# Attention's rounds: parts turned ahead of the projection, their copies ahead of the exponentials, small copies dealt to other engines

## The chip, the core and the metric

The kernel runs on one core of a Trainium2 chip. The metric is the device time in microseconds (us), the median of several runs; before the change it is 1904.55 us (three runs, 1902.47 to 1905.32). The engines are named as the profile names them: PE is the matrix engine, PEld its loading of weights, DVE the vector engine, ACT the scalar engine, POOL GpSimd, SP the queue that issues the transfers.

## What is computed

A hybrid block of transformer parts, all in float32, on x of 4 x 256 tokens with 512 features:

```python
x = x + attention(layernorm(x))   # 32 heads of 16, rotary, causal, plus 10 adapter keys and values
x = x + ffn(layernorm(x))         # x @ weight.T + bias, kept only where clusters are hit
x = x + ssd_mixer(layernorm(x))   # in_proj, conv of 4 taps, state-space mixer of 128 heads, gate, norm, out_proj
x = x + ffn(layernorm(x))         # the same weights again
return x
```

In attention, queries and keys are projected and rotated, `scores = q k / 4` are masked causally, a softmax follows, and its weights meet the values. The adapter's keys and values, projected with the same weights from 10 rows, add a second, separate softmax times a gate. The sum goes through `w_proj`. The change lies in attention and in the first feed-forward, which is woven into attention's last rounds. The mixer, which takes most of the time, is not edited.

## The kernel before, in words

**Precision.** A product in float32 is made of three matmuls [...]: each operand is split into a high half (a rounded copy) and a low half (the rest). `split` (L102) makes the two, the high one on ACT (L104), the low one on DVE or POOL (L105). `mm3` (L107) issues the three matmuls for each of 4 blocks of 128 features (L112 to L114), so a projection of one tile of 128 tokens is 12 matmuls. 16 numbers of a head are stacked as high and low halves to a depth of 64, so that scores come from single matmuls on "parts".

**Attention's rounds.** The loop of L658 has 32 rounds, i = 0 to 31. Each is four heads (u = i mod 8) of one batch (b = i div 8), and queries and keys of 256 tokens. Work of several ages meets in a round, in this order of TensorE:

1. `scores(b, u)` (L429): 8 matmuls of parts into four PSUM tiles `sc` (L443), then 4 matmuls that add the mask (L450). DVE takes the negative maxima `nmx` (L455), ACT the exponentials with their sums into `e` (L458), eight instructions.
2. In even rounds but the first the first half of `adapter_scores` (L401): 4 matmuls into `pa`; ACT copies it to `sa` (L409).
3. `step("long", i)`: projections that are due. `prepared` (L360) lists those of the next batch: two query and two key projections and two of values for its two tiles of tokens; each q or k is then rotated by DVE (L281 to L285) and summed to `r` on POOL (L287); values are copied by ACT (L385). The number `r` in `prepared` (L363) is the round at which the first of them is due, and each takes the next round. For the first batch it is negative, and what falls below zero is done ahead of the loop. Projections of attention's output (`closed`, L546) and of the feed-forward (`fed`, L583) are due in the same way.
4. Parts (second half of `pieces`, L387): 8 transposes `trp` (L395), then two copies to `pc` (L397), on DVE for queries (f = 0) and on ACT for keys (f = 1).
5. `step("values", i)`, for some rounds the adapter's values `pya` (L540).
6. `weigh` of round i-2 (L477): exponentials that were turned before, times values, to `py`; ACT copies `py` to `ys` (L494).
7. `turn` of round i-1 (L464): 12 transposes of `e` into three tiles `ptr` (L473); they are copied to `eT` (L474), the first two on DVE and the third on ACT.
8. `gathered` of round i-3 (L497): two transposes `try` (L500), then the division by the sums on DVE; then the second half of the adapter's scores, `tra` (L413).
9. `step("turn", i)`: transposes that are due: normalised tiles (`tr`, L163, whose halves are `axs`), output rows (`try`, L557), the adapter's weights (`pt`, L531), at the start the adapter's keys (`tra`, L336).
10. First half of `pieces` for a later round: `stacked` (L301) writes the high halves into a stack `st` with a copy that is repeated twice, on ACT (L305), and the low halves with a subtraction on POOL (L306). There are two stacks for queries and two for keys, and a part uses both of its kind; rounds alternate between queries and keys.

**PSUM.** Projections, `trp`, `pa`, `ptr`, `try`, `tra`, `tr` and the like share three buffers of tag "m". Scores have four of their own, `py` one.

**What sets the order.** On TensorE the loop's order is as written (`manual_schedule`, L657). The instructions of other engines are put in order by the framework's planner when the program is built: each has a priority from its place in the program, and among those that its own model of time has ready the earliest goes first. [...] `tc.high_priority(offset=60)` moves what is written in its block ahead in priority by 60 places.

**The stage's end.** After the loop the last rounds are finished by hand (L713 to L747): the last output projections, and the feed-forward for the tiles of tokens 3 to 7. Tiles 6 and 7 are normalised, both turned (L744), then both fed (L747).

## Time and profile before

| What | us |
|---|---|
| median of 3 runs | 1904.55 |
| the profiled execution | 1905.57 |
| its span, first to last instruction | 1903.8 |
| ahead of attention's rounds | 0 to 33 |
| rounds 0 to 31 of attention, and what follows round 31 at once | 33 to 350 |
| the rest of attention and of the first feed-forward | 350 to 385 |
| mixer and second feed-forward | 385 to 1904 |

A line of the groups view gives line, engine, operation and tiles, then busy time, the mean of one in ns, and the idle time ahead of it with what ended it. The groups that matter between 40 and 345 us, by that view:

| Group | count | mean ns |
|---|---|---|
| L458 ACT exponential, 128x256 and 128x128 | 248 | 430 |
| L458 ACT reading of the sum after each | 248 | 217 |
| L455 DVE maximum | 124 | 546 |
| L473 PE transposes of exponentials | 384 | 285 |
| L474 copies to eT: DVE, ACT | 64, 32 | 684, 597 |
| L397 copies to pc: DVE, ACT | 30, 30 | 678, 627 |
| L305 ACT copies to st | 56 | 447 |
| L306 POOL subtractions to st | 56 | 458 |
| L494 ACT copies to ys | 31 | 404 |

Matmuls overlap in the array, so the duration of one (0.39 us for 512 columns) is longer than the distance to the next (0.235 us). The distance is what counts for the sum.

### The profile page before, as it was taken

Reading aid. Unit: us, or ns where it says so; the run is one execution under the profiler, and the core shown is the slowest. Engines: PE = TensorE matmul, PEld = TensorE weight load, DVE = VectorE, ACT = ScalarE, POOL = GpSimd, SP = SyncE. Lnnn points to the kernel's source line nnn. Section 1 sums busy time; section 2 is a strip of 40 time slices with the busy share of each in tenths; the row PEclk is TensorE's granted clock in tenths of the full one; section 3 lists DMA queues with packets and bytes.
Section 4 is the critical chain, followed back from the end, with each engine's and each line's share of the span. In section 5 each row is a group of like instructions: output and inputs, shape, how many; then the busy total and the mean of one; then the engine's idle time right before and its main releaser. Section 6 shows DMA issues by size and latency. Waiting matters only on the chain.

```text
span 1903.8 us, 29900 instructions
## 1 busy us (share of the span) xinstructions
PE 1815.8 (95%) x10690; PEld 1453.8 (76%) x10690; DVE 1473.3 (77%) x2319; ACT 1379.9 (72%) x2874; POOL 346.9 (18%) x312
## 2 busy tenths in 40 slices
PE   7989888889999999999999999999999999999997
PEld 5767666767777887878788788777787888787786
DVE  5466667588998778777877797778778877877777
ACT  4676687368898767867877787678777776786753
POOL 4221120011321211121112121210221121111100
PEclk8999999999999999999999999999999999999999
DMA  3000000025555454554445454545554444455341
GB/s 132 11 1 1 22 14 1 22 66 173 171 186 180 155 166 144 162 165 150 157 159 161 144 188 137 177 144 168 150 167 142 158 155 161 147 159 170 112 124 49
DMA packets 151909, 240.35 MB, mean 126 GB/s; under 512 B 12368, under 2 KB 77520, under 8 KB 151760
## 3 DMA queue, kind: packets, MB, share of 16 engines
q1 hardware_dynamic: 151760, 238.44, 39.3%
q8 instruction: 84, 1.38, 0.3%
q14 instruction: 65, 0.53, 0.1%
HBM read 202.75 MB, written 35.65 MB: 125 GB/s over the span
## 4 chain that ended last, share of the span: by engine, by line
PE 73%; ACT 12%; DVE 8%; DMA 3%; issue 3%; POOL 1%; SPq 0%; ACTq 0%; DVEq 0%; POOLq 0%
PE pp L112 12%; PE pp L113 11%; PE pp L114 11%; PE pyy L1016 8%; PE pog L112 6%; PE pog L114 6%; PE pog L113 6%; ACT e L458 4%; PE trx L1001 3%; DMA wor<-in_wout_dram 1%; PE ptr L473 1%; DVE acc L942 1%; ACT L946 1%; PE pg L956 1%; ACT acc L946 1%
## 5 line engine op out<-in xcount | busy, mean ns | idle before, releaser
L112 PE MATMUL pp<-mx,w 128*128 128x512 f32 (+1 forms) x1160 | 465.1, 401 | 9.1 <-DVE acc L942 8.6
L114 PE MATMUL pp<-mx,w 128*128 128x512 f32 (+1 forms) x1160 | 454.1, 391 | 0.0
L113 PE MATMUL pp<-mx,w 128*128 128x512 f32 (+1 forms) x1160 | 453.9, 391 | 0.0
L942 DVE SCALAR_TENSOR_TENSOR acc<-pp,cw_s,acc 128x1012 f32<-128x1012 f32 (+2 forms) x240 | 304.9, 1270 | 22.9 <-ACT acc L935 22.3
L990 DVE TENSOR_TENSOR em<-em,gm 128x1536 f32<-128x1536 f32 x128 | 229.7, 1795 | 94.3 <-ACT em L984 86.0
L112 PEld LDWEIGHTS pp<-mx,w 128*128 128x128 f32 x1160 | 218.2, 188 | 66.9 <-issue 11.0
L114 PEld LDWEIGHTS pp<-mx,w 128*128 128x128 f32 x1160 | 218.4, 188 | 45.5 <-issue 0.4
L113 PEld LDWEIGHTS pp<-mx,w 128*128 128x128 f32 x1160 | 218.6, 188 | 40.8 <-issue 0.7
L1039 POOL TENSOR_TENSOR sq<-sq,acc 128x1024 f32<-128x1024 f32 x55 | 132.5, 2409 | 583.1 <-ACT acc L1038 583.1
L104 ACT CAST w<-wr 128x512 fp32r<-128x512 f32 x144 | 88.5, 615 | 189.0 <-PE pp L113 154.2
L978 POOL TENSOR_SCALAR_AFFINE_SELECT r<-r 128x512 f32<-128x512 f32 x128 | 125.1, 977 | 548.9 <-DMA r<-cumd 484.6
L112 PE MATMUL pog<-wo,gh 128*128 128x512 f32 x512 | 204.4, 399 | 0.0
L983 ACT ACTIVATE em<-r,col_t 128x128 f32<-128x128 f32 x512 | 164.9, 391 | 48.7 <-PE pyy L1016 48.4
L114 PE MATMUL pog<-wo,gh 128*128 128x512 f32 x512 | 200.2, 391 | 0.0
L113 PE MATMUL pog<-wo,gh 128*128 128x512 f32 x512 | 199.9, 390 | 0.0
L1016 PE MATMUL pyy<-em,xd 128*64 128x256 f32 (+1 forms) x2048 | 189.1, 329 | 2.9 <-DVE em L990 2.9
L1016 PEld LDWEIGHTS pyy<-em,xd 128*64 128x64 f32 x2048 | 134.0, 137 | 64.4 <-issue 20.4
L986 ACT ACTIVATE em<-r,col_t 128x128 f32<-128x128 f32 x512 | 166.5, 388 | 0.0
L974 DVE TENSOR_SCALAR em<-r,col_t 128x128 f32<-128x128 f32 x512 | 137.7, 328 | 12.6 <-PE pyy L1016 10.1
L1002 DVE TENSOR_TENSOR xd<-trx,dt_t 128x512 f32<-128x512 f32 x128 | 86.1, 682 | 53.7 <-PE trx L1001 53.6
L458 ACT ACTIVATE e<-sc,nmx 128x256 f32<-128x256 f32 (+1 forms) x256 | 103.5, 430 | 31.3 <-DVE nmx L455 31.3
L105 DVE TENSOR_TENSOR w<-wr,w 128x512 fp32r<-128x512 f32 x139 | 98.2, 708 | 34.5 <-ACT w L104 34.4
(287 smaller groups left out, 3187.9 us busy)
## 6 DMA issues: line engine op xcount, KB each, us to landing
wr<-in_win_dram SPq DMA_DIRECT2D x287, 256.0 KB, 2.8
r<-cumd SPq DMA_DIRECT2D x128, 512.0 KB, 4.2
spill<-gb SPq DMA_DIRECT2D x63, 512.0 KB, 2.8
gr<-spill SPq DMA_DIRECT2D x120, 256.0 KB, 3.3
wor<-in_wout_dram SPq DMA_DIRECT2D x64, 256.0 KB, 3.2
out_dram<-x SPq DMA_DIRECT2D x8, 256.0 KB, 2.3
x<-in_x_dram SPq DMA_DIRECT2D x1, 1536.0 KB, 9.5
gr<-spill SPq DMA_DIRECT2D x8, 192.0 KB, 2.6
```

What stands on the lines that cost most here:

```text
L112: nc.tensor.matmul(o, lh, rh, start=(first and k == 0), stop=False)
L113: nc.tensor.matmul(o, lh, rl, start=False, stop=False)
L114: nc.tensor.matmul(o, ll, rh, start=False, stop=(last and k == n - 1))
L458: nc.scalar.activation(es_[c][:, 2 * j + pr, :], sc[:, j, :], AF.Exp, bias=nm[:, j : j + 1], accum_out=rs[:, c, h : h + 1],)
L942: nc.vector.scalar_tensor_tensor(av[:, :, d:], pv[:, :, : L - d], cw_s[:, ch, tap : tap + 1], av[:, :, d:], ALU.mult, ALU.add,)
L974: nc.vector.tensor_scalar(e[:, b, 2, :], rv[:, b, 1, :], col_t[:, h, b, 1:2], 0.0, ALU.subtract, ALU.min,)
L978: nc.gpsimd.affine_select(rv[:, :, 0, :], rv[:, :, 0, :], pattern=[[0, B], [1, P]], compare_op=ALU.is_ge, fill=-1e30, base=0, channel_mult ...
L983: nc.scalar.activation(e[:, b, 1, :], rv[:, b, 1, :], AF.Exp, bias=col_t[:, h, b, 2:3])
L986: nc.scalar.activation(e[:, b, 0, :], rv[:, b, 0, :], AF.Exp, bias=col_t[:, h, b, 0:1])
L990: nc.vector.tensor_tensor(e, e, gm, ALU.mult)
L1016: nc.tensor.matmul(py[d, b, k * P :], xd[:, 2 * b + k, d], es2[hh][:, b, 2 * k : 2 if k == 0 else 3, :].rearrange("p s i -> p (s i)"), sta ...
L1039: (nc.gpsimd if n < NB - 1 else nc.vector).tensor_tensor(sq, sq, x2, ALU.add)
```

## The change

It has these parts, all but the last two in the rounds:

- `scores` becomes a generator: its first half ends after the maxima, its second half has the exponentials.
- In a round, the parts are turned (point 4 above) after point 2 and ahead of the exponentials and of `step("long", i)`. So the order is scores, adapter, parts, exponentials, projections, values and so on.
- Both kinds of parts are copied to `pc` by ACT.
- Of the turned exponentials, the one of the first 128 queries (first in order) is copied by ACT, the two others by DVE.
- `ys` is copied by DVE in place of ACT.
- The high halves in `stacked` are copied by POOL in place of ACT.
- The first batch's list starts at -6 in place of -5, the second's at 1 in place of 0: one value projection more is done ahead of the loop, and those of the second batch come one round later.
- In `fed`, a tile's normalising and turning get a priority that is 60 places ahead.
- At the stage's end tile 6 is turned and fed, then tile 7.

```diff
@@ stacked
-                nc.scalar.copy(st[:n, :, HI[f], :], v.to_broadcast([n, 8, 2, HD]))
+                nc.gpsimd.tensor_copy(st[:n, :, HI[f], :], v.to_broadcast([n, 8, 2, HD]))
@@ prepared
-                r = 8 * (b - 1) if b else -5
+                r = {0: -6, 1: 1}.get(b, 8 * (b - 1))
@@ pieces
-                    nc.scalar.copy(o[:, :, cs], tr) if f else nc.vector.tensor_copy(o[:, :, cs], tr)
+                    nc.scalar.copy(o[:, :, cs], tr)
@@ scores
-                made = []
+                made, tops = [], []
...
                     nc.vector.tensor_reduce(nm, sc, AX.X, ALU.max, negate=True)
+                    tops.append(nm)
+                yield
+                for (c, pr, sc), nm in zip(made, tops):
                     for j in range(2):
                         h = 4 * u + 2 * j + pr
                         nc.scalar.activation(
...
-                return es_
+                all_es[8 * b + u] = es_
+                yield
@@ turn
-                    nc.scalar.copy(dst, pt) if k else nc.vector.tensor_copy(dst, pt)
+                    nc.scalar.copy(dst, pt) if src is es_[0] else nc.vector.tensor_copy(dst, pt)
@@ weigh
-                nc.scalar.copy(ys, py)
+                nc.vector.tensor_copy(ys, py)
@@ fed
-                xs = normed(f.norm, t)
+                with tc.high_priority(offset=60):
+                    xs = normed(f.norm, t)
@@ the loop
-                    es_[i] = scores(b, u)
+                    scoring = scores(b, u)
+                    next(scoring)
...
-                    step("long", i)
                     if part:
                         next(part)
                     part = None
+                    next(scoring)
+                    step("long", i)
                     step("values", i)
...
-                        eTs[i - 1] = turn(es_.pop(i - 1))
+                        eTs[i - 1] = turn(all_es.pop(i - 1))
@@ the end
                     feed.norm.turn(xn, tr, xs)
-                    late[t] = xs
-                for t, xs in late.items():
                     feed.tile(t, xs, [ps_s.tile([P, FH], F32, name="pd", tag="sc") for _ in range(2)])
```

More of the change, by code (lines that the diff above doesn't have):

```diff
@@ L624, in attention @@
             n = B * 8
-            es_, eTs, yss = {}, {}, {}
+            all_es, eTs, yss = {}, {}, {}
             feed = None
@@ L715, in attention @@
                 yss[n - 2] = weigh(b, 6, eTs.pop(n - 2))
-                eTs[n - 1] = turn(es_.pop(n - 1))
+                eTs[n - 1] = turn(all_es.pop(n - 1))
                 gathered(b, 5, yss.pop(n - 3))
```

## The prediction

> **What bounds the kernel now.** I read the page first, its busy shares, slices and chain:

> ```profile
> PE 1815.8 (95%) x10690; PEld 1453.8 (76%) x10690; DVE 1473.3 (77%) x2319; ACT 1379.9 (72%) x2874; POOL 346.9 (18%) x312
> PE   7989888889999999999999999999999999999997
> PEclk8999999999999999999999999999999999999999
> PE 73%; ACT 12%; DVE 8%; DMA 3%; issue 3%; POOL 1%; SPq 0%; ACTq 0%; DVEq 0%; POOLq 0%
> ```

> TensorE sets the time. The slices below 9 are the first nine, and those are attention. The table by stage (us, then busy time of PE, PEld, DVE, ACT, POOL, then the clock) says how much can be won:

> ```profile
> 33.00:130.00 97.00, 86.10 (x630) 67.50 (x631) 53.73 (x110) 65.45 (x242) 24.99 (x36) 0.92 0.04 12
> 130.00:262.00 132.00, 120.69 (x1003) 94.18 (x1002) 86.73 (x187) 89.47 (x331) 28.52 (x41) 1.00 0.05 13
> 262.00:350.00 88.00, 74.50 (x659) 60.27 (x658) 60.49 (x147) 59.77 (x207) 9.88 (x16) 0.96 0.04 13
> 385.00:1904.00 1519.00, 1486.64 (x8161) 1192.40 (x8159) 1228.99 (x1762) 1137.50 (x2043) 264.10 (x191) 0.99 0.48 151
> ```

> From 33 to 350 us PE idles 35.7 of 317 us (10.9+11.3+13.5), and no other engine is full: ACT 68%, DVE 63%, POOL 20%. The mixer after 385 isn't touched. Then the waits of PE alone in 33 to 350 (total us, times, longest):

> ```profile
> PE ptr L473 <- ACT pc L397: 5.6, 5, 1.6
> PE trp L395 <- ACT sa L409: 4.5, 6, 1.0
> PE ptr L473 <- DVE pc L397: 3.6, 3, 2.0
> PE pd L112 <- ACT axs L104: 3.6, 2, 2.8
> PE tra L413 <- ACT eT L474: 3.3, 9, 0.5
> PE pya L540 <- ACT pc L397: 2.4, 2, 1.2
> ```

> Most are waits for a PSUM buffer of tag "m" (three of them) that a copy has not yet emptied, and the copy stands behind the exponentials on ACT. The timeline shows it, in round 4 (80 to 89 us) and in round 7:

> ```profile
> 84.88 0.38 ACT L409 COPY sa<-pa 80x256 f32<-80x256 f32 x1
> ...
> 85.41 0.51 PE L395 MATMUL trp<-con,st 128*128 128x128 f32 x4 [0.64 <-ACT sa L409]
> ...
> 88.90 0.36 PE L413 MATMUL tra<-con,sa 80*128 80x80 f32 x2 [0.39 <-ACT eT L474]
> ...
> 112.03 1.11 ACT L397 CAST pc<-trp 128x512 fp32r<-128x512 f32 x2
> 112.70 0.66 PE L473 MATMUL ptr<-con,e 128*128 128x128 f32 x4 [1.58 <-ACT pc L397]
> ```

> pa was complete at 81.5, but its copy came at 84.9, after eight exponentials (81.7 to 84.9), and PE lost 0.8 us. In round 7, which has no projection as cover, PE lost 1.8 us twice.

> [...] after the waits before 33 us a projection's matmuls start 0.43 us apart until 38.9, then 0.235; the same at 58 to 62 and 114 to 118 us. So a long wait costs some 2 us more afterwards. [...] L306 on POOL takes 449 to 467 ns in all 64 full-size cases[...]. [...] 128x512 from PSUM takes 681 ns on DVE (L474) and 586 on ACT.

> **The change, part by part.** A projection occupies PE for 2.8 us (81.52 to 84.32), scores and masks 1.0, a part's turning 0.75, values 0.8, the three turns of exponentials 1.45, the way back 0.35; pa and tra of even rounds 0.55 and 0.3. So a round with a projection holds 7.1 us (odd) or 8.0 us (even) of PE work. The starts of scores in the timeline (72.60, 79.98, 89.19, 96.58, 105.56, 113.51 for rounds 3 to 8) give 7.4 for odd and 9.2 and 9.0 for even rounds: the even ones have 1.0 to 1.2 us to give.

> *Order.* Turning a part right after the scores, its two copies (0.63 each on ACT) ahead of the exponentials. ACT runs sa 0.38, pc 1.25, exponentials 3.35: they end some 6.1 us (odd) or 6.5 (even) after the round's start, 1.2 to 1.5 later than now. The projection (1.75 to 4.6 us of the round) covers that. sa is empty about when the second turning ends, so the buffer for the projection is ready. Worked round by round against the starts in the timeline:
> - Even rounds with a projection: 4, 10, 12, 18, 20, 28 give 0.95 to 1.2 each (6.65), 6, 14, 22 and 30 0.15 to 0.5 (1.3): **-8.0**.
> - Rounds in which values or turns wait for pc: 9 and 17 give 1.5 each, 15 and 23 0.7, 25 0.6, 29 0.9: **-5.9**.
> - Odd rounds 3, 5, 11, 19: already near full, 0.2 to 0.35 each: -1.15. Rounds 13 and 21 project values, whose copy (0.62, ACT) comes behind the later exponentials: +0.3 each. Sum **-0.6**.
> - Rounds without a projection (8, 16, 24, 26, 27) have no cover. The late exponentials and the turn's first copy behind them (end near 7.1) hold the next buffer, unless that is taken from a DVE copy. Round 27 takes 6.25 now, 26 takes 7.8, 16 takes 8.3. I take +0.7, +0.2, +0.5, and -0.5 and -0.9 for 8 and 24, which now also pay for a cold clock or for copies ahead of their exponentials: **0**.
> - Round 2's cold clock (2 us now) halved: **-1.0**. Round 31 waits 2.8 for axs behind late exponentials; the feed's higher priority can take axs ahead: -2.5 to 0, I take **-1.0**.

> *The shifted projections* (first index -6 and 1). One value projection (2.8) goes ahead of the rounds, where PE waits 5.5 us for parts (trp on POOL's st, two waits). It hides there, but turnings then come later and the stacks (two for each of q and k) pass that on through POOL: rounds start 1.5 later. Round 0 keeps two projections, less cold: -1.0. Round 1 loses both, 5.6 of PE work, and becomes bound by ACT and the adapter's keys: -5.6+1.5. Round 7 gains one, whose 2.8 fill its 3.4 of waits: 8.4 instead of 7.95, +0.45. Sum **-3.2**.

> *Copies dealt anew*, over 32 rounds: st (64 and 4 copies) leaves ACT for POOL, -29.3 on ACT (64 x 0.433 + 4 x 0.398); the parts of q (32) go from DVE to ACT, +20.1 on ACT (x 0.628), -21.7 on DVE (x 0.678); ys (32) from ACT to DVE, -12.7 on ACT (x 0.396), about +13.1 on DVE by the 128x256 row at 0.41 (L284). ACT -21.9, DVE -8.6: off the path by themselves, their effect is in the rounds above. The turn's copies stay two DVE, one ACT, but ACT has the first. The POOL copy of 128x256 isn't in the trace: a cast of half that width took 0.29 (L610) and once 0.787 (L611), a memset of 8 columns 0.104. Taking 0.1 fixed and 0.19 for 128 columns: 0.48. [...] Ends: 0.31 (memset's rate) and 1.57 (twice 0.787). Two copies and two subtractions are 1.9 us, on an engine that now waits for ACT's st (117 us of waits). They hide, if POOL runs them in the round before: it can, since ACT now issues st as soon as the stack is free (85.14 in round 4, for a part turned two rounds later). No SP or DMA queue is moved past.

> *End of the stage.* Turn and feed of tile 6 now come ahead of tile 7's turn. PE waits 3.1 there (tr on axn), but tile 6's low half comes on DVE only at 369.97, after that axn; and tile 7's split is then no longer hidden (1.3). **0**, between -2 and +2.

> Sum -8.0-5.9-0.6-1.0-1.0-3.2 = -19.7. Copies put in places where a slot or a queue is a little late give some back; for that I take 1.7, about what PE waits now in the smaller lines of its list: **-18.0**. The profiled execution took 1905.57 (span 1903.8 and 1.8 around it): 1887.6. It lies 1.0 above the median of 1904.55, so I forecast **1887**.

> **The rivals.** *A, as worked out*: 1887, by itself 1875 to 1896; 0.62. *B, the wait is exchanged*: exponentials end 1.2 to 1.5 us later and the turn's first copy stands behind them, so the some 20 rounds with projections lose 0.6 each by a wait of try or tra for eT: -18+12, **1899**. For it: PE waits for eT already (3.3 us). Against: DVE's copies give earlier buffers. 0.20. *C, slower*: the parts are turned 2.8 us earlier in the round than now, so st must be ready 1.0 us after its start. If POOL runs the four st instructions only where they are written, at the end of the round, each of 29 rounds waits 1.9-1.0, with PE uncovered: +26-18 = +8, **1913**. It decides from 18/29 = 0.62 us a round. For it: [...] the sum r (1.28) can stand ahead. Against: the early issue above. 0.12. *D, the order of ACT stays*: only PE's order is fixed by hand; if the planner still puts exponentials first, the buffers stay late, and the shifted projections alone give 3: **1902**; 0.06.

> **How the numbers follow.** A fills 1875 to 1896; the low end 1873 adds the bounds of round 31 and the stage's end. B takes the range up to 1903, leaving out C and a little of each: about 2 in 10. A measurement can tell about 0.2% (3.8 us) from no change. Faster by more: A and most of B, 0.78. Within: rest of B and D, 0.10. Slower: C, 0.12.

> **What would show it.** Right: sa and pc stand before or among the first exponentials; PE no longer waits for sa (4.5) or pc (11.6 in three lines); even rounds take 8.0 to 8.3; L305 shows POOL at about 0.48; PE idle in the stage falls from 36 to some 20 us. B: a long line of try or tra for ACT eT. C: trp for POOL st grows past 10 us. Wrong altogether: a time after 385 that differs by more than 2 us, as nothing in the mixer changes.

## The result and the profile after

The changed kernel takes 1895.27 us, median of 5 runs (1892.93 to 1898.48), against 1904.55 of the kernel before; the ratio is 0.9953, 95% interval 0.9938 to 0.9967. It is 9.3 us faster, where 17.5 were forecast.

The page of the changed kernel, the lines that answer to those shown before:

```profile
PE 1816.5 (96%) x10690; PEld 1453.2 (77%) x10690; DVE 1465.8 (77%) x2319; ACT 1367.5 (72%) x2808; POOL 389.9 (21%) x380
PE   7999988799999999999999999999999999999997
PEclk8999999999999999999999999999999999999999
PE 76%; ACT 8%; DVE 8%; DMA 3%; issue 3%; POOL 1%; SPq 0%; DVEq 0%; ACTq 0%; POOLq 0%
```

PE has the same work in a shorter span. A slice is 47.4 us: the third, fifth and ninth have gained a tenth, and the eighth (331 to 379 us), the end of the stage, has lost one. ACT's share of the chain fell from 12% to 8%. The table by stage, with the windows moved by 10 us where attention ends earlier:

```profile
33.00:130.00 97.00, 89.28 (x704) 69.98 (x707) 56.45 (x121) 66.55 (x241) 38.30 (x70) 0.95 0.04 12
130.00:262.00 132.00, 121.42 (x1011) 94.33 (x1003) 85.89 (x193) 87.62 (x313) 43.07 (x72) 0.99 0.05 13
262.00:340.00 78.00, 67.62 (x572) 54.43 (x571) 52.09 (x135) 46.27 (x163) 7.65 (x16) 0.93 0.05 14
375.00:1894.00 1519.00, 1487.22 (x8161) 1192.90 (x8161) 1229.42 (x1764) 1141.61 (x2048) 281.12 (x191) 0.99 0.47 151
```

PE idles 28.7 us from 33 to 340 (7.7+10.6+10.4), where it was 35.7 from 33 to 350 before; some 20 were expected. The waits of PE in 33 to 350:

```profile
PE pd L112 <- ACT axs L104: 3.1, 3, 2.2
PE pq L112 <- ACT sa L409: 3.0, 8, 0.7
PE try L504 <- ACT eT L478: 2.8, 2, 1.7
PE pt L535 <- ACT eT L478: 2.6, 2, 2.3
PE try L504 <- DVE eT L478: 2.5, 6, 0.8
PE tra L413 <- DVE eT L478: 1.8, 6, 1.0
PE ptr L477 <- ACT av L385: 1.6, 1, 1.6
```

The waits for pc by ptr and pya (11.6) are gone, as forecast. The wait for sa is not: the projection pq has taken it over from trp (8 waits, 3.0). The waits for eT have grown: all lines of them together from 9.1 to 12.3, those for ACT's eT from 4.0 to 6.6. Round 4 of the changed kernel in the timeline:

```profile
72.65 0.81 PE L395 MATMUL trp<-con,st 128*128 128x128 f32 x8
72.85 0.48 ACT L461 ACTIVATE e<-sc,nmx 128x256 f32<-128x256 f32 x1 [2.14 <-DVE nmx L455]
...
73.32 0.35 ACT L409 COPY sa<-pa 80x256 f32<-80x256 f32 x1
73.57 1.07 ACT L397 CAST pc<-trp 128x512 fp32r<-128x512 f32 x2
...
73.72 0.51 PE L112 MATMUL pq<-wq,axs 128*128 128x512 f32 x1 [0.26 <-ACT sa L409]
```

Parts are turned early and their copies stand ahead of seven of eight exponentials. But one exponential stands ahead of sa, and PE, through with the parts at 73.46, begins the projection at 73.72. The projection waits for sa because it needs a buffer of tag "m", and the three are held by pa and the two trp.

Two readings serve for all that follows. One is the **stage end**, the start of the matmul L226 that closes the first feed-forward: 381.5 us before, 372.0 after, a difference of 9.5. What follows it took 1522.3 us in both profiled executions, and 1518 to 1524 in those of the experiments, although nothing is edited there. So the stage end shows an edit in attention better than the total of one run does. It is that of one traced execution for each kernel, though; against the medians of all executions, the gain over the kernel before by the stage end is up to 4 us smaller (with sa ahead) and up to 2.6 larger (the copies alone). The other is the length of a round, from the start of its scores to that of the next; rounds of the same kind in different batches (4, 12 and 20; 9 and 17) agree within 0.1, mostly within 0.03, where the clock is the same.

### The profile page after: what moved, and what is told of

Its sections match the earlier page's. It is cut to its first block, busy times and chain, and to the rows that moved or that the text cites. A ratio compares the mean times of both kernels' runs of the same rounds, so it can differ in the third digit from the quotient of the medians.

```text
span 1894.3 us, 29853 instructions
## 1 busy us (share of the span) xinstructions
PE 1816.5 (96%) x10690; PEld 1453.2 (77%) x10690; DVE 1465.8 (77%) x2319; ACT 1367.5 (72%) x2808; POOL 389.9 (21%) x380
## 4 chain that ended last, share of the span: by engine, by line
PE 76%; ACT 8%; DVE 8%; DMA 3%; issue 3%; POOL 1%; SPq 0%; DVEq 0%; ACTq 0%; POOLq 0%
PE pp L112 12%; PE pp L113 11%; PE pp L114 11%; PE pyy L1021 8%; PE pog L112 6%; PE pog L114 6%; PE pog L113 6%; PE trx L1006 3%; ACT e L461 2%; DMA wor<-in_wout_dram 2%; DVE acc L947 1%; PE ptr L477 1%; PE pq L112 1%; PE pq L113 1%; PE pq L114 1%
## 5 line engine op out<-in xcount | busy, mean ns | idle before, releaser
L112 PE MATMUL pp<-mx,w 128*128 128x512 f32 (+1 forms) x1160 | 465.2, 401 | 8.1 <-DVE acc L947 7.6
L112 PEld LDWEIGHTS pp<-mx,w 128*128 128x128 f32 x1160 | 218.3, 188 | 65.6 <-issue 10.4
L983 POOL TENSOR_SCALAR_AFFINE_SELECT r<-r 128x512 f32<-128x512 f32 x128 | 141.5, 1106 | 532.1 <-DMA r<-cumd 452.2
L104 ACT CAST w<-wr 128x512 fp32r<-128x512 f32 x144 | 88.4, 615 | 186.9 <-PE pp L113 148.1
L112 PE MATMUL pog<-wo,gh 128*128 128x512 f32 x512 | 204.5, 399 | 0.0
## 6 DMA issues: line engine op xcount, KB each, us to landing
x<-in_x_dram SPq DMA_DIRECT2D x1, 1536.0 KB, 10.9
```

The costliest lines, as they stand in the source:

```text
L112: nc.tensor.matmul(o, lh, rh, start=(first and k == 0), stop=False)
L983: nc.gpsimd.affine_select(rv[:, :, 0, :], rv[:, :, 0, :], pattern=[[0, B], [1, P]], compare_op=ALU.is_ge, fill=-1e30, base=0, channel_mult ...
```

## The experiments

The first theory was that the shifted projections bring most of the gain, and that waits for buffers had kept their size and changed their place (theory 1 below). The rival was the prediction's own split of the gain (theory 2). Every ratio is to the kernel before, measured beside the experiment, with its 95% interval.

**The shift alone**, on the kernel before:

```diff
-                r = 8 * (b - 1) if b else -5
+                r = {0: -6, 1: 1}.get(b, 8 * (b - 1))
```

> The kernel before with one edit alone: the first batch's projections start at -6, the second's at 1. The reading is the start of the matmul L226, the end of attention and the first feed-forward: 381.5 us before, 372.0 after the whole change. Theory 1 (the shift fills idle PE ahead of the rounds and in round 7, and frees round 1; it brings most of the gain): 374 to 375, some 0.9963 of the time before. Theory 2 (the prediction's sizes: the shift gives 3, the order gives 14 and loses it elsewhere): 378 to 379, 0.998.

Measured: stage end 381.2, ratio 0.9987 (0.9981 to 0.9993). Rounds 0 and 1 give 4.1, rounds 2, 3, 7 and 9 take 3.5 back (round 7 is 1.0 longer, with a projection more in it), and rounds 24 and 25 1.5. In the kernel before, round 8 ran at a clock of 0.81 and round 9 at 1.00; how much of what these two changed is the clock's was not shown. The stage gains 0.3. The medians differ by 2.5; in the two traced executions 4.0 lie behind the stage's end, where nothing is edited, and why is open. Theory 1 falls, and by the stage end theory 2's 3.2 isn't there either.

**The order of a round alone**, copies, start and end as before:

```diff
-                    step("long", i)
                     if part:
                         next(part)
                     part = None
+                    next(scoring)
+                    step("long", i)
```

> The kernel before with the new order of a round alone (parts turned first, exponentials after them, then the projection), all copies on the engines of before, no shift, the old end. Theory 1 (waits for buffers change their place and nearly keep their size): stage ends at 378 to 380. Theory 2 (the order gives 14, and the copies dealt anew lose it): 367 to 369.

Measured: stage end 374.9, ratio 0.9961 (0.9948 to 0.9974). The order gives 6.6: between the theories. Round 7 falls from 7.95 to 5.34, 9 and 17 from 11.47 to 10.18, 15 from 8.43 to 7.47; but the even rounds 4, 12 and 20 only from 9.20 to 8.9, and 14 and 22 grow by 0.3 to 0.4. Round 8, behind the short round 7, takes 1.5 back.

**The copies alone**, in the old order and with the old start and end. One thing is not as before: the exponentials are written after the adapter's copy sa, so sa has priority over them.

```diff
-                    if part:
-                        next(part)
-                    part = None
                     next(scoring)
                     step("long", i)
+                    if part:
+                        next(part)
+                    part = None
```

> The change with the old order of a round, the old start of the projections and the old end: only the copies are dealt anew (st on POOL, both parts on ACT, ys on DVE, the turn's first on ACT). Theory 1 (copies off the path, but pc of queries now stands behind the exponentials too): stage ends at 380 to 384. Theory 2 (the new deal costs the order's gain): 388 or later.

Measured: stage end 383.9, ratio 1.0025 (1.0018 to 1.0033), in the range of theory 1. Without the new order the new deal costs 2.3 in the stage, since all pc copies now stand behind exponentials:

```profile
PE ptr L477 <- ACT pc L397: 18.7, 13, 3.9
```

But its even rounds 4, 12 and 20 take 8.02, of which PE is busy for 7.96, where the change takes 8.54. In this kernel sa stands behind the first exponential too; the projection comes after pa and before the parts, and so it has a buffer when it starts. That pointed to sa.

**The old end of the stage** in the changed kernel:

```diff
-                with tc.high_priority(offset=60):
-                    xs = normed(f.norm, t)
+                xs = normed(f.norm, t)
...
                     feed.norm.turn(xn, tr, xs)
-                    feed.tile(t, xs, [ps_s.tile([P, FH], F32, name="pd", tag="sc") for _ in range(2)])
+                    late[t] = xs
+                for t, xs in late.items():
+                    feed.tile(t, xs, [ps_s.tile([P, FH], F32, name="pd", tag="sc") for _ in range(2)])
```

> The change without its last two edits: tiles 6 and 7 are both turned, then both fed, and normalising in the feed has its plain priority. From the start of round 31 to L226 it takes 56.6 us before and 58.6 after. If the new end costs those 2 us: 56.6 and a stage end at 370. If they come from the copies and the order of round 31: 58 to 59, stage end 371.5 to 372.5.

Measured: from round 31 to L226 55.9 us, stage end 370.4, ratio 0.9922 (0.9906 to 0.9938). The two edits together cost 2.7 in that stretch. PE's idle time there differs by only 0.4 (11.5 and 11.1); the rest is the same 320 matmuls taking longer, and the changed kernel has one more piece of 3.4 us at half clock, 361.0 to 364.4 (0.50 there, and 0.91 over the stretch in place of 0.94), behind the wait shown below. That piece can account for up to 1.7, by an estimate: half of its length. In the thirteen kernels with the old end the stretch takes 55.8 to 57.2, so by this comparison the new end costs at least 1.4; which of its two edits does was not tried. Without them round 31 starts 1.1 later, though: rounds 0 and 1 are 1.8 longer, at a clock of 0.72 and 0.85 in place of 0.81 and 1.00. In the changed kernel the end's wait of 3.1 for axn has become one for the split of tile 6, and a second, smaller one for that of tile 7:

```profile
359.05 0.40 PE L112 MATMUL pd<-fw,axs 128*128 128x288 f32 x1 [2.83 <-ACT axs L104]
...
365.84 0.40 PE L112 MATMUL pd<-fw,axs 128*128 128x288 f32 x1 [0.73 <-ACT axs L104]
```

With the old end, tile 7's turn waits for axn once, and behind 340 us PE waits for splits 0.2 us in all on ACT, in place of 3.8:

```profile
360.49 0.66 PE L163 MATMUL tr<-con,axn 128*128 128x128 f32 x4 [3.14 <-DVE axn L155]
```

This version, with 370.4, is the base of all experiments below. They were measured at other times on other chips than the base. By the intervals of the ratio only those with sa ahead reach no higher than the base's lower end (0.9906 to 0.9938); for the others the reading is the stage end and the rounds.

**sa ahead of the exponentials.** `adapter_scores` yields the copy's instruction:

```diff
-                    next(scoring)
+                    with tc.issue_after(lead) if lead is not None else ExitStack():
+                        next(scoring)
```

> The change with the old end of the stage, and the exponentials of an even round bound to stand behind the adapter's copy sa on ACT (so far one exponential stands ahead of it). If even rounds lose their time because the projection waits for sa's buffer behind one exponential: 8.54 falls to 8.0 to 8.15 in rounds 4, 6, 12 and 20, the wait of pq for sa (2.9 us) goes, stage ends at 367 to 368 in place of 370.4. If another wait takes its place (pc, or eT at the end of the round): rounds stay at 8.4 or more and the stage ends at 370 or later.

Measured: stage end 363.5, ratio 0.9884 (0.9868 to 0.9901). Rounds 4, 12 and 20 take 8.11 to 8.16, round 6 8.10. Nine even rounds (4, 6, 10, 12, 14, 18, 20, 22, 28) give 0.4 to 0.8 each, 4.9 in all, and the line of pq for sa is gone. Round 4 again:

```profile
73.98 0.37 ACT L409 COPY sa<-pa 80x256 f32<-80x256 f32 x1 [2.21 <-PE pa L405]
74.25 0.47 ACT L461 ACTIVATE e<-sc,nmx 128x256 f32<-128x256 f32 x1
74.40 0.50 PE L112 MATMUL pq<-wq,axs 128*128 128x512 f32 x1
```

No wait stands at pq any more. The gain is larger than expected (367 to 368): the waits for sa of these nine rounds summed to 3.55 in the base (2.93 of pq, 0.62 of po in round 28), and each round gives 0.1 to 0.2 more than its wait was. Rounds 8 and 25 give 2.3 more, and that is the clock's: they take 1.25 and 1.05 less, with the same program order on PE. The start and the other rounds take 0.3 back. The windows of rounds 8 and 25, base first, then with sa ahead (the clock is the number before the last two):

```profile
105.57:114.70 9.13, 8.39 (x69) 6.47 (x69) 5.08 (x12) 6.49 (x23) 1.65 (x4) 0.81 0.00 1
260.71:269.48 8.77, 7.47 (x68) 6.13 (x68) 3.26 (x7) 6.52 (x23) 1.64 (x4) 0.86 0.01 2
```

```profile
104.54:112.41 7.87, 7.02 (x69) 5.38 (x69) 5.06 (x12) 5.84 (x23) 1.66 (x4) 1.00 0.00 1
255.07:262.78 7.71, 6.41 (x67) 5.27 (x66) 3.25 (x7) 6.52 (x23) 1.64 (x4) 1.00 0.01 2
```

So before reading a difference of 1 us in a round as the edit's, look at its clock.

**ys on ACT again.**

```diff
-                nc.vector.tensor_copy(ys, py)
+                nc.scalar.copy(ys, py)
```

> The change with the old end of the stage, and ys copied by ACT again. If ys on DVE delays the copies of turned exponentials behind it (try and tra wait 2.5 and 1.9 for DVE's eT): stage ends at 368 to 369 in place of 370.4. If ACT is the tighter one, because ys then stands ahead of the turn's first copy behind the exponentials: 371 to 373.

Measured: stage end 368.9, ratio 0.9917 (0.9902 to 0.9931). Of the 1.45 gained, 1.0 is round 8, whose clock is 1.00 here and 0.81 in the base, and 0.84 is round 0, at 0.81 in place of 0.72. That is more than the whole; rounds 13, 15, 16, 21, 24 and 25 lose 0.25 to 0.28 each. So the stage end lies in the first expectation's range, but not for its reason, and the deal of ys is worth nothing either way that can be told.

**The old deal of the turn's copies.**

```diff
-                    nc.scalar.copy(dst, pt) if src is es_[0] else nc.vector.tensor_copy(dst, pt)
+                    nc.scalar.copy(dst, pt) if k else nc.vector.tensor_copy(dst, pt)
```

> The change with the old end of the stage, and the turn's copies dealt as before (the first two on DVE, the third on ACT). If the first copy on ACT, behind the exponentials, holds the next buffer (try, pt and try2 wait 2.8, 2.6 and 0.9 for ACT's eT): rounds 23 and 24 lose 1.5 to 2 each, stage ends at 366 to 368 in place of 370.4. If the deal is right because DVE has the maxima and ys ahead: 371 to 374.

Measured: stage end 364.4, ratio 0.9904 (0.989 to 0.9919). Of the 6.0 gained, 3.8 are there when round 2 starts, with rounds 0 and 1 at clock 1.00 (0.72 and 0.85 in the base), and rounds 8 and 25 give 1.27 and 1.53, also at clock 1.00 (0.81 and 0.86 in the base). The deal's own mark is on two rounds: 23, at clock 1.00 in both, gives 1.76, and 15 gives 0.69; these are rounds where the prediction had a gain and the change a loss. In round 23 of the changed kernel (first line; the base has the same wait, 1.68) the way back waits for the turn's first copy, which ACT reaches after all exponentials; with the old deal it waits less, for a copy of DVE:

```profile
249.49 0.44 PE L504 MATMUL try<-con,ys 128*128 128x128 f32 x2 [1.69 <-ACT eT L478]
```

```profile
246.64 0.44 PE L504 MATMUL try<-con,ys 128*128 128x128 f32 x2 [0.80 <-DVE eT L478]
```

Round 24 gives nothing, against what was expected. Nine rounds with a projection pay 0.3 to 0.4 each (3 to 5, 11, 12, 14, 19, 20, 22), 3.3 together. That is more than rounds 15 and 23 give, so the 6.0 are mostly start and clock, and the deal itself is about even.

**No shift.**

```diff
-                r = {0: -6, 1: 1}.get(b, 8 * (b - 1))
+                r = 8 * (b - 1) if b else -5
```

> The change with the old end of the stage and without the shift of the projections. Together with the order alone (374.9, neither shift nor copies) and the change with the old end (370.4, both) it parts shift and copies. If the shift is worth little in this order too (alone it gave 0.3): 370 to 371, and the copies give 4 to 5. If it is the shift that gives it, by relieving round 1 (8.45 in place of 13.98 in the order alone): 374 or later.

Measured: stage end 372.5, ratio 0.9945 (0.993 to 0.996). This lies between the two expectations. So in this order the shift is worth 2.1: round 1 grows by 5.2 and the rounds start 1.6 later, but round 7, without its projection, is 3.2 shorter. Round 25 is 1.0 shorter too, by its clock alone (1.00, base 0.86). With the order alone (374.9) that makes a sum in one line: order 6.6, copies 374.9-372.5 = 2.4, shift 372.5-370.4 = 2.1, new end -1.6; together the 9.5; a round's clock, 1.25 us in round 8 with sa ahead, is in each term.

**Both gains together.** With sa ahead as above, ACT takes the turn's first copy in rounds with a projection alone:

```diff
-                        eTs[i - 1] = turn(all_es.pop(i - 1))
+                        eTs[i - 1] = turn(all_es.pop(i - 1), 2 <= i < 28 and i % 8 not in (0, 7) and i not in (25, 26, 27))
```

> The change with the old end of the stage, the exponentials of even rounds behind sa, and the turn's first copy on ACT in rounds with a projection alone (2 to 27 without u = 0, u = 7, 25, 26, 27); in the others the third is ACT's, as before. If the two gains seen apart (6.9 for sa first, 6.0 for the old deal) lie in different rounds save 8, 25 and 28, and the mixed deal also spares the 0.38 that the old deal costs in rounds with a projection: stage ends at 357 to 360, total some 25 us under the kernel before, 0.986 to 0.988. If they are the same waits: 362 to 363.

Measured: stage end 359.6, total 1880.46, ratio 0.9878 (0.9859 to 0.9897), as expected. It is faster than both kernels: 23 us under the kernel before, measured side by side. Rounds 23 (9.10, 1.0 above the old deal's 8.14) and 24 (10.10) remain the weak ones.

**sa ahead, with the old deal of the turn's copies** in all rounds:

> As the one before, with the old deal of the turn's copies in all rounds. If the old deal costs 0.38 in rounds with a projection because ACT's third copy holds the buffer of tra or try: rounds 3 to 6, 11 to 14 and 18 to 22 take 0.3 to 0.4 more than in the mixed deal, stage ends at 361 to 363. If sa first has freed ACT so that this is gone: within 1 us of the mixed deal.

Measured: stage end 360.9, ratio 0.9888 (0.9869 to 0.9906). Rounds 3, 4, 11, 12, 14, 19, 20 and 22 take 0.35 to 0.4 more than in the mixed deal, but 13, 18 and 21 some 0.1 or less, and round 23 is 1.0 shorter, so neither expectation holds fully: the mixed deal is 1.4 ahead by the stage end, and their totals can't be told apart.

**The stacks on ACT.**

```diff
-                nc.gpsimd.tensor_copy(st[:n, :, HI[f], :], v.to_broadcast([n, 8, 2, HD]))
+                nc.scalar.copy(st[:n, :, HI[f], :], v.to_broadcast([n, 8, 2, HD]))
```

> The change with the old end of the stage, and the stacks' high halves copied by ACT again. If POOL takes 29 us from an ACT that paces many rounds: stage ends 2 to 5 later than 370.4. If these copies only fill idle time of ACT: 370 to 371. If the POOL copy (0.40) delays the parts: earlier than 370.

Measured: stage end 370.8, ratio 0.9955 (0.9938 to 0.9973). That is the range for copies that only fill idle time, but by the clock. Without the 2.3 that rounds 8 and 25 gain at clock 1.00 (0.81 and 0.86 in the base), the copies on ACT cost 2.8, as much as round 1 does (11.21 in place of 8.45, at about the same clock, 0.87 and 0.85), where the adapter's keys go through the stacks. From round 2 to 22, save round 8 and 0.3 in 9 and 17, the rounds are the same to 0.1: the copies that the change took from ACT, 29 us over the stage, changed nothing in those rounds.

**The parts of queries on DVE.**

```diff
-                    nc.scalar.copy(o[:, :, cs], tr)
+                    nc.scalar.copy(o[:, :, cs], tr) if f else nc.vector.tensor_copy(o[:, :, cs], tr)
```

> The change with the old end of the stage, and the parts of queries copied by DVE again. They stand among the maxima there; on ACT they delay the exponentials by 1.1 in every second round. If the late exponentials cost more: stage ends at 367 to 369. If the maxima, delayed by 1.3, hold the exponentials as well: 370 to 372.

Measured: stage end 361.5, ratio 0.9903 (0.9886 to 0.9919), better than either expectation by the stage end. Rounds 2 to 7 and 9 to 22 are unchanged (0.04 at most, round 2 0.2). Rounds 8 and 25 give 2.3 by their clock, 1.00 in place of 0.81 and 0.86, and round 27, which ran at 0.79 in the changed kernel, 1.2. The rest is the start: the rounds start 1.75 earlier, and rounds 0 and 1 give 3.1, at clock 1.00 in place of 0.72 and 0.85. Ahead of the rounds, PE waits for the stacks in the base twice (0.84 and 2.10), here once:

```profile
31.13 0.75 PE L395 MATMUL trp<-con,st 128*128 128x128 f32 x4 [2.10 <-POOL st L306]
```

```profile
29.59 0.54 PE L395 MATMUL trp<-con,st 128*128 128x128 f32 x4 [1.18 <-POOL st L306]
```

The scores of round 0 wait 0.68 for pc in both. So in the steady rounds the deal of pc is free. At the start it goes with a shorter wait and a full clock; which of the two brings how much of the 5 was not separated. That deal with sa ahead was not tried.

## Why the prediction came out as it did

The sign and the range were right, the size was twice too large, and the place was right only in that it is attention. Of the 9.5 us by the stage end, 8.6 were gained by the start of round 2, where the prediction's terms sum to 3.6. From there on 0.9 came, where its terms sum to 16.1. That half of the forecast came at all is luck in good part: the start gave 5.0 more than forecast, the rounds behind it 15 less. By its steps, in lengths of rounds:

- **Even rounds with a projection, -8.0: measured -1.0.** This is the step that failed. It said that sa is empty about when the second turning ends. The turning ended at 73.46 in round 4, but sa left ACT at 73.67, some 0.4 later than it could have: pa was complete at 72.8, and one exponential (72.85, 0.48) was run first. The order in the program doesn't bind ACT, though sa is written ahead of the exponentials; that the planner's model has the first of them ready before pa is likely, but not on record. With sa bound ahead of it these rounds gave 4.9 more, -6.0 in all against the kernel before. The rest stays open; in part it is round 30, 0.7 longer than before, which the old deal of the turn's copies shortens by 0.4. The page's 4.5 us of trp for sa was not removed but became 3.0 of pq for sa, because the early parts had used up the cover that the projection had been.
- **Rounds in which values or turns wait for pc, -5.9: measured -1.1.** The mechanism held where nothing else waits: rounds 9 and 17 gave 1.46 and 1.43 (1.5 forecast), 29 0.71 (0.9). Rounds 15, 23 and 25 lost 0.07, 1.33 and 1.07 where 0.7, 0.7 and 0.6 were to be gained: the old deal shows for 15 and 23 that the cause is the turn's first copy on ACT, and round 25 fell from clock 1.00 to 0.86, which alone cost 1.05 in the comparison above. The prediction had this wait, but only for rounds without a projection and in rival B.
- **Odd rounds, -0.6: measured -1.2**; 13 and 21 gave 0.13 and 0.15 instead of losing 0.3. **Rounds without a projection, 0: measured -0.5.**
- **Start and round 7, -3.2: measured -7.6**, of it -8.6 by the start of round 2 (+0.3 ahead of the rounds, -2.1 in round 0, -6.8 in round 1) and +1.0 in round 7 (+0.45 forecast). The sum of the whole change hides here what the parts show: order, POOL's stacks and shift meet in round 1. From 14.42, the shift alone takes it to 11.31, the order alone to 13.98, and the copies alone lengthen it to 16.70; all together halve it (7.63). Its clock is part of that: 1.00, and 0.92 before.
- **Round 2, -1.0: -0.1**, the clock stayed low (0.84, then 0.88). **Round 31 and the end, -1.0 and 0: +2.0**, at the bound that the prediction gave for the end. The old end shows that it is these two edits, with a piece at half clock as part of it.
- **POOL's copy, 0.48: measured 0.398 (median)**, hidden as forecast: after round 1 PE nowhere waits for st; ahead of the rounds it does, 2.7 in place of 5.5. Rival C, parts that come late, is out. Rival D is true of one exponential in eight, which stands ahead of both sa and pc. Rival B's mechanism is there, in some rounds and not in twenty: the waits for eT grew by 3.2, where it had 12.

The smaller lines for which 1.7 were given back had no measurement of their own.

## What to carry to other kernels

Moving a step ahead of the work that covered it moves its wait too: ask what the next step needs, and whether that copy is really ahead in its engine's queue, since here the order in the program did not put it there and an explicit edge did. Taking 29 us of copies off ACT, which was 72% busy, gave nothing in the steady rounds; the place of a single copy of 0.4 us in its queue gave 4.9. Undo a bundle's parts one by one: here the new end cost time, and the shift, worth 0.3 alone, was worth 2.1 in company.

## What was not expected of the hardware

The clock of PE at rounds 8 and 25 changed with edits that keep PE's order there: it was 0.81 and 0.86 in the base, and in the eight kernels built on it 1.00 in round 8 of all and in round 25 of seven. With the same order of matmuls that was 1.25 and 1.05 us of a round, less than the 2 that the prediction estimated for what follows a long wait. Round 0 ran at anything from 0.69 to 1.00.

```profile
102.79:106.20 3.41, 1.82 (x19) 1.34 (x18) 1.43 (x3) 2.41 (x11) 0.43 (x1) 1.00 0.00 0
106.20:109.62 3.42, 3.42 (x26) 2.87 (x28) 2.31 (x6) 1.98 (x6) 0.94 (x3) 0.50 0.01 2
```

With sa ahead the grid cuts the wait in two, PE is busy for 0.78 and 0.76 of the two pieces in place of 0.53, and the clock stays at 1.00:

```profile
99.49:102.91 3.42, 2.68 (x28) 1.65 (x26) 2.31 (x5) 3.42 (x17) 1.76 (x2) 1.00 0.00 0
102.91:106.32 3.41, 2.58 (x26) 2.31 (x26) 1.85 (x5) 1.30 (x5) 0.00 (x0) 1.00 0.00 0
```

So an edit that ended this wait 1 us earlier came with 1.25 us less in a round whose order on PE it didn't touch. The grid lies differently in these traces: counted from the span's start, the border next to 104 us falls at 104.07 before, at 105.03 in the changed kernel, at 102.79 in the base and at 102.91 with sa ahead. There is one trace of each kernel; the mean clock of 41 executions of the kernel before ran from 0.983 to 0.990. Whether round 8 keeps its clock over executions of one kernel is thus not shown.

A 128x256 copy that repeats its source took 398 ns on POOL in the changed kernel and 433 on ACT in the kernel before (medians of 64); a subtraction of half its width took 460 and 457 on POOL.
